# Other halves for the first exponentials, another order for the first loads, norms and masks, and turns of the identity at the start

## The chip, the cores and the metric

The kernel runs on one core of a Trainium2 chip. The metric is the time of one launch on the device in microseconds; times of single instructions come from one profiled execution of the same kernel.

## What is computed

Eight batches of x (256 channels by 512 positions) get a masked cross-attention with 16 heads of 16 channels against a context, and then a feed-forward part with a shared and eight routed experts. The reference, cut to what matters here (x and the context are indexed channel by position):

```python
q = einsum('oc,bct->bot', Wq, layernorm(x)) + bq      # k, v: the same with Wk, Wv on the context
dot = einsum('bhdt,bhds->bhts', q, k) / 4
mask = m[:, :, :, None] * m[:, :, None, :]
dot = mask * dot - (1 - mask) * 1e6
amap = softmax(dot, -1) * mask
x = x + einsum('bhts,bhds->bhdt', amap, v)
n = layernorm(x)
x = x + n + shared_expert(n) + routed_experts(n)      # two of eight experts a row
```

## The kernel before

The order of all work is written out by hand: each engine carries out its instructions in the order in which the code issues them, and waits where an operand or a buffer is not ready. Heads are taken in groups of four, four groups G to a batch, so G runs from 0 to 31. The products are in fp32.

**Setup (lines 115 to 194 and 1002 to 1026).** SyncE's queue (SP) issues the loads of x of batch 0 in two halves, then four small loads of the biases into bnat, then the context ctx. ScalarE's queue (ACT) issues Wq, the mask mb spread over all partitions, Wk and Wv. GpSimd (POOL) makes the identity ident and then a row of constants, the last of them nm, which takes the row maxima. `square` (line 1005) turns a weight matrix on TensorE, four turns of 128x128 into PSUM, and ACT copies it out. VectorE makes the layer norm of x in xm (`norm_stats` at 328, POOL raises the variance to -1/2 in rs, `start_norm` at 350 subtracts, scales and masks) and masks the context (`mask_context`, 341). `row_terms` (214) turns the biases and makes alpha and beta, with which `extra_rows` (385) gives each q and k its rows for bias and mask. `project_qk` (398) multiplies by the turned weights (psq, psk), and VectorE writes the two tiles of a pair of groups, one for each a in 0 and 1 (`rows`, line 409).

**Row maxima of group 0 (1034 to 1050).** `row_max` (421) makes the scores of 128 queries for half a group, that is for two heads, each on 32 rows of TensorE (L427), into PSUM tile s1 or s2, and VectorE takes the maximum (L429). Between the eight of them stand the turn of the mask (L1046), the router's weights (`load_router`, 253, L258) and seven tiles of shared weights (`weight_thunks`, 261, L272 and L284), each copied out by ACT. These and psq, psk take their PSUM from a pool with two buffers, tag mm; tags long, s1, s2 and av have one each. Then `take_max` (434) turns the maxima (psn, L438) and VectorE subtracts them from q (L439).

**Steps (1071 to 1146).** Each group has eight steps h. A step issues a `row_max` of the next group (L427 and L429, always into s1), `exp_scores` of this one (443: scores the other way round on two heads' rows, L450, into s2, and ACT's exponential, L452), at even h `attend` (457, av), and pieces of other work: `project_v` (360, psv, L372), `project_qk` of group pairs to come, loads, and later the feed-forward part. From step 6 of group 0 on, the maxima run LEAD = 2 steps ahead and the two matmul calls of a step are on different halves, that is on different rows of TensorE; in steps 1 to 5 of group 0 they run one ahead, and both calls are on the same half. In step 5 two maxima are issued to catch up.

## Time and profile before

| | us |
|---|---|
| median of 3 runs (911.38 to 923.37) | 920.09 |
| profiled execution | 898.62 |
| its span, first to last instruction | 896.8 |
| first k tile of group 0 ready (end of L411's third) | 14.5 |
| first row maximum's matmuls begin (L427) | 14.6 |
| q of group 0 less its maxima ready (L439) | 29.7 |
| matmuls of step 7 of group 0 end | 62.5 |

The three runs lie up to 1.3% apart. In the profile PE is TensorE's matmuls and PEld its weight loads, DVE is VectorE; L427 is line 427 of the kernel. "128x1024" is partitions by elements. The granted clock (PEclk) is TensorE's, as a share of full speed. A name left of "<-" is written, one right of it read; in a row of waits it is what ended the wait. Some rows from the beginning that the text uses:

| line, engine, operation | mean ns |
|---|---|
| L429 DVE maximum of 128x1024 | 1224 |
| L452 ACT exponential of 128x1024 | 1023 |
| L411 DVE q or k tile, 128x512 | 746 |
| L439 DVE subtraction from q, 128x512 | 688 |
| L393 ACT extra row, 128x512 | 810 |
| L344 POOL ctx times mask, 128x512 (later batches) | 1273 |
| L873 POOL issue of a load (later) | 609 |

### The profile page before, as it was taken

The page shows a single profiled execution, that of the slowest core. Times are in us where ns is not written, and L with a number is a line of the kernel's source. Part 1 is how long each engine was busy: PE and PEld are TensorE (multiplying, and loading weights), DVE is VectorE, ACT ScalarE, POOL GpSimd, SP SyncE. Part 2 cuts the span into 40 slices and gives each one's busy share as a digit, 9 for nine tenths or more (in the row PEclk, how much of TensorE's full clock was granted, in tenths as well). Part 3 has the DMA queues.
Part 4 walks back from the last instruction along what each step waited for, and adds up shares of the span by engine and source line. Part 5 has one row for each costly group of instructions (what it writes and reads, how often), then busy time and mean ns, then how long its engine had stood idle before and what let it go on. Part 6 is the DMA issues. An engine that isn't in the chain of part 4 may idle for free.

```text
span 896.8 us, 13356 instructions
## 1 busy us (share of the span) xinstructions
PE 844.5 (94%) x4947; PEld 340.3 (38%) x4947; DVE 580.9 (65%) x1083; ACT 364.3 (41%) x474; POOL 317.9 (35%) x393
## 2 busy tenths in 40 slices
PE   6998989999999999999999999999999998999996
PEld 3332323333333333333333333333333333555553
DVE  6556767776777677767776778577867753432356
ACT  3224444443444344434443444344434441455540
POOL 2105303552355235523552344234421121344431
PEclk9799999999999999999999999999999998999998
DMA  6119903212671255125512510020000001455455
GB/s 178 36 39 362 343 20 86 33 35 50 130 90 35 50 137 83 35 51 136 83 35 50 125 30 19 19 71 1 19 19 12 7 18 41 108 136 141 118 182 194
DMA packets 93004, 75.31 MB, mean 84 GB/s; under 512 B 60328, under 2 KB 81347, under 8 KB 92556
## 3 DMA queue, kind: packets, MB, share of 16 engines
q1 hardware_dynamic: 84956, 50.04, 21.3%
q0 software_dynamic: 7024, 23.37, 11.4%
q10 hardware_dynamic: 960, 1.05, 0.4%
q8 instruction: 40, 0.66, 0.3%
q14 instruction: 24, 0.20, 0.1%
HBM read 38.10 MB, written 40.79 MB: 88 GB/s over the span
## 4 chain that ended last, share of the span: by engine, by line
PE 72%; DVE 16%; issue 5%; POOL 3%; DMA 2%; SPq 1%; ACT 0%; DVEq 0%; ACTq 0%; POOLq 0%
PE s L427 23%; DVE nm L429 9%; PE av L465 9%; PE psy L956 4%; PE eu L793 4%; PE psq L404 4%; PE pu L905 3%; PE eg L793 3%; PE ey L823 3%; PE psk L404 3%; PE psv L372 3%; PE s L450 3%; PE pgu L905 3%; PE pg L905 2%; DVE q L411 2%
## 5 line engine op out<-in xcount | busy, mean ns | idle before, releaser
L452 ACT ACTIVATE e<-s 128x1024 f32<-128x1024 f32 x256 | 262.0, 1024 | 407.5 <-PE s L450 407.3
L429 DVE TENSOR_REDUCE nm<-s 128x2 f32<-128x1024 f32 x256 | 313.3, 1224 | 144.8 <-PE s L450 129.7
L427 PE MATMUL s<-k,q 32*128 32x512 f32 x1024 | 290.9, 644 | 24.3 <-DVE nm L429 21.3
L450 PE MATMUL s<-q,k 32*128 32x512 f32 x1024 | 289.9, 642 | 1.5 <-DVE q L439 0.8
L465 PE MATMUL av<-e,V 128*32 128x512 f32 x1024 | 137.5, 605 | 0.2 <-ACT e L452 0.2
L427 PEld LDWEIGHTS s<-k,q 32*128 32x128 f32 x1024 | 77.0, 184 | 131.7 <-DVE nm L429 110.4
L395 POOL TENSOR_SCALAR extra<-mb,alpha,beta 128x512 f32<-128x512 f32 x60 | 45.5, 763 | 175.9 <-DVE q L411 175.6
L337 POOL TENSOR_TENSOR rs<-ve,mhalf 128x1 f32<-128x1 f32 x32 | 18.2, 569 | 209.0 <-DVE ve L335 209.0
L450 PEld LDWEIGHTS s<-q,k 32*128 32x128 f32 x1024 | 77.3, 184 | 7.8 <-issue 5.6
L799 DVE SCALAR_TENSOR_TENSOR hz<-eth,eu 128x352 bf16<-128x352 f32 x45 | 23.4, 521 | 56.7 <-PE eu L793 49.3
L465 PEld LDWEIGHTS av<-e,V 128*32 128x32 f32 x1024 | 20.4, 108 | 98.1 <-issue 94.7
L956 PE MATMUL psy<-sdT,h 128*128 128x512 f32 (+1 forms) x96 | 52.3, 665 | 2.3 <-DVE h L917 2.3
L206 POOL DMA_INDIRECT xs<-xnb,at x30 | 29.9, 997 | 50.0 <-DVE at L654 27.2
L905 PE MATMUL pu<-xT,sguT 128*128 128x256 f32 x128 | 36.7, 403 | 0.0
L372 PE MATMUL psv<-WvT,ctx 128*128 128x256 f32 x128 | 36.7, 411 | 0.0
L793 PEld LDWEIGHTS <-late_ctx 128*128 128x128 bf16 x296 | 27.6, 97 | 23.4 <-issue 5.3
L905 PE MATMUL pg<-xT,sguT 128*128 128x256 f32 x128 | 35.3, 401 | 0.0
L793 PE MATMUL eu<-guT,late_ctx 128*128 x148 | 34.1, 310 | 0.9 <-ACT eth L798 0.8
L404 PE MATMUL psq<-xm,WqT 128*128 128x512 f32 x64 | 34.2, 660 | 0.0
L905 PE MATMUL pgu<-xT,sguT 128*96 128x256 f32 (+1 forms) x128 | 34.1, 393 | 0.0
L411 DVE SCALAR_TENSOR_TENSOR q<-psq,mine,extra 128x512 f32<-128x512 f32 x32 | 22.6, 746 | 15.6 <-PE psq L404 15.6
L206 POOL DMA_INDIRECT whose<-who,at x30 | 28.8, 961 | 9.1 <-issue 8.8
(200 smaller groups left out, 973.9 us busy)
## 6 DMA issues: line engine op xcount, KB each, us to landing
xs<-blank SPq DMA_DIRECT2D x7, 1920.0 KB, 13.2
ctx<-in_ctx_dram SPq DMA_DIRECT2D x8, 512.0 KB, 5.4
z<-zs SPq DMA_DIRECT2D x15, 256.0 KB, 4.5
x<-in_x_dram SPq DMA_DIRECT2D x7, 512.0 KB, 3.7
accd<-acc SPq DMA_DIRECT2D x12, 256.0 KB, 2.2
again<-accd POOLq DMA_DIRECT2D x12, 256.0 KB, 3.6
out_dram<-again POOLq DMA_DIRECT2D x12, 256.0 KB, 4.2
gu<-in_L_ffn_w_gate_dram POOLq DMA_DIRECT2D x8, 352.0 KB, 4.4
```

The source lines that it names most:

```text
L206: i = nc.gpsimd.indirect_dma_start(to[:, :], bass.IndirectOffsetOnAxis(ap=rows, axis=0), what, None, **bounds).ins
L372: nc.tensor.matmul(ps, ct[:, kc, sc * P : (sc + 1) * P], WvT[:, kc, :], start=(kc == 0), stop=(kc == 1))
L395: engine.tensor_scalar(t, S[b]["mb"], at, be, ALU.mult, ALU.add)
L404: nc.tensor.matmul(ps, W[:, kc, g // 2].rearrange("p j a d -> p (j a d)"), rhs[:, kc, :], start=(kc == 0), stop=(kc == 1),)
L427: nc.tensor.matmul(ps[:, jj, :], q[r, tci * P : (tci + 1) * P], k[r, :], start=True, stop=True)
L429: best = lambda: nc.vector.reduce_max(NM[G % 2][:, tci, c0 : c0 + 33 : 32], ps, axis=AX.X)
L450: nc.tensor.matmul(ps[:, jj, :], k[r, sc * P : (sc + 1) * P], q[r, :], start=True, stop=True)
L452: nc.scalar.activation(e, ps, AF.Exp)
L465: nc.tensor.matmul(AVT[G][32 * j : 32 * j + 32, :], V[:, sc, 2 * g + j // 2, j % 2 : j % 2 + 2, :].rearrange("p o d -> p (o d)"), et[j // ...
L793: nc.tensor.matmul(ps, xT[:, kc, :], weights_of(t, guT, m, kc, slice(None)), start=(kc == 0), stop=(kc == NKC - 1),)
L905: lambda kc=kc: nc.tensor.matmul(ps, sguT[:, m, kc, i0 : i0 + n + more], s["xT"][:, kc, :], start=(kc == 0), stop=(kc == NKC - 1))
L956: nc.tensor.matmul(t["y"], t["h"][:n, ic, tt * P : (tt + 1) * P], sdT[:n, ic, :], start=(ic == 0), stop=(ic == 2))
```

## The change

Five things, all at the beginning:

- The loads: ACT issues mb first, then Wk, Wq, Wv; SP issues x in halves and then ctx; the four loads of the biases go to POOL, after the identity. POOL's constants and nm are made after its part of the setup.
- Norms and masks: xm is made in one VectorE operation a half (subtract the mean, times mask), and ACT multiplies by rs. POOL masks one half of ctx, VectorE the other. `row_terms` is split: what does not need the biases is made in terms first, and `bias_terms` adds the biases.
- TensorE turns the identity into a PSUM tile that nobody reads (`busy`), 15 times at the start, and 2, 3 and 6 times between the first products.
- q's product for group pair 0 is issued in two parts with other work between. Of q and k the tiles for a = 0 are made first; q's for a = 1 comes after the first row maximum, k's after the second. The turned mask takes tag long. `project_v(0, 0)` is issued before the first exponentials; the others at steps 0, 5 and 7.
- Steps 1 to 5 of group 0: the exponentials take the other half than before (`half` for `1 - half`, steps 0 to 5), and the second maximum of step 5 comes at the end of that step.

```diff
+    nc.scalar.dma_start(out=S[0]["mb"], in_=mask[0, 0].partition_broadcast(P))
     for i in range(2):
         nc.sync.dma_start(out=S[0]["x"][:, i, :], in_=x[0, i * P : (i + 1) * P, :])
-    wq_nat = load_square(Wq)
-    nc.scalar.dma_start(out=S[0]["mb"], in_=mask[0, 0].partition_broadcast(P))
+    wk_nat, wq_nat = load_square(Wk), load_square(Wq)
+    nc.sync.dma_start(out=S[0]["ctx"], in_=src[0].rearrange("(h p) t -> p h t", p=P))
+    wv_nat = load_square(Wv)
...
-            nc.sync.dma_start(out=bnat[row : row + 2, :, a, :], in_=by_group[a])
-    nc.sync.dma_start(out=S[0]["ctx"], in_=src[0].rearrange("(h p) t -> p h t", p=P))
-    wk_nat, wv_nat = load_square(Wk), load_square(Wv)
+            nc.gpsimd.dma_start(out=bnat[row : row + 2, :, a, :], in_=by_group[a])
...
+    def busy(n):
+        for _ in range(n):
+            nc.tensor.transpose(idle, ident, ident)
+
+    idle = ps_av.tile([P, P], F32, tag="av", name="idle")
...
-    square(wq_nat, WqT, 0.25, ps_m, "mm")
-    start_norm(0, nc.vector)
+    def normed(i):
+        start_stats(0, i)
+        mv, rs = s0["stats", i]
+        xm = s0["xm"][:, i, :]
+        nc.vector.scalar_tensor_tensor(xm, s0["x"][:, i, :], mv[:, 0:1], s0["mb"], ALU.subtract, ALU.mult)
+        return lambda: nc.scalar.mul(xm, xm, rs)
+
+    row_terms()
+    busy(15)
     square(wk_nat, WkT, 1.0, ps_s, "s1")
-    row_terms()
-    mask_context(0, nc.vector)
-    wv = turn_square(wv_nat, ps_s, "s2")
-    extra_rows(0, 0, nc.scalar)
+    square(wq_nat, WqT, 0.25, ps_s, "s2")
+    busy(2)
+    scaled = normed(0)
+    scaled()
+    q_part, q_rows = project_qk(0, 0, True)
+    k_part, k_rows = project_qk(0, 1, True)
+    q_part(0)
+    scaled = normed(1)
+    bias_terms()
+    nc.gpsimd.tensor_mul(s0["ctx"][:, 0, :], s0["ctx"][:, 0, :], s0["mb"])
+    nc.vector.tensor_mul(s0["ctx"][:, 1, :], s0["ctx"][:, 1, :], s0["mb"])
+    scaled()
+    wv = turn_square(wv_nat, ps_s, "s1")
+    extra_rows(0, 0, nc.scalar, (0,))
+    extra_rows(0, 1, nc.scalar, (0,))
+    busy(3)
+    q_part(1)
+    q_rows(0)
+    for kc in range(2):
+        k_part(kc)
+    k_rows(0)
+    busy(6)
+    extra_rows(0, 0, nc.scalar, (1,))
     nc.scalar.copy(WvT, wv)
-    extra_rows(0, 1, nc.scalar)
-    project_qk(0, 0)
-    k_rows = project_qk(0, 1, True)
+    extra_rows(0, 1, nc.scalar, (1,))
...
             best = row_max(1, 0, 0, "s1", True)
             take_max(0)
+            best()
+            project_v(0, 0)
+            continue
         best()
         if r == 0:
-            k_rows(1)
-            pt = ps_m.tile([P, B * 4], F32, tag="mm", name="pt")
+            q_rows(1)
+            pt = ps_m.tile([P, B * 4], F32, tag="long", name="pt", bufs=1)
...
+        elif r == 1:
+            k_rows(1)
             load_router()
-        elif r != 7:
+        if r not in (0, 7):
             weights.pop(0)[1]()
...
-                lead = LEAD if G or h > 5 else LEAD - 1
-                for R in range(8 * (G + 1) + h + lead, 8 * (G + 1) + h + lead + (2 if G == 0 and h == 5 else 1)):
-                    if (G or h) and R // 8 < last:
-                        row_max(R // 8, (R % 8) // 2, R % 2)
-                exp_scores(G, st, 1 - half, "s2" if R // 8 < last else ("s1", "s2")[h % 2])
+                short = G == 0 and h < 6
+                R = 8 * (G + 1) + h + LEAD - short
+                if (G or h) and R // 8 < last:
+                    row_max(R // 8, (R % 8) // 2, R % 2)
+                exp_scores(G, st, half if short else 1 - half, "s2" if R // 8 < last else ("s1", "s2")[h % 2])
...
-                if b == 0 and g == 0 and h in (0, 2, 5, 7):
-                    project_v(0, (0, 2, 5, 7).index(h))
+                if b == 0 and g == 0 and h in (0, 5, 7):
+                    project_v(0, (0, 5, 7).index(h) + 1)
...
+                if G == 0 and h == 5:
+                    row_max(1, 3, 1)
```

More of the change, by code (lines that the diff above doesn't have):

```diff
@@ L125, in xattn_ffn_kernel @@
     }
+    nc.scalar.dma_start(out=S[0]["mb"], in_=mask[0, 0].partition_broadcast(P))
     for i in range(2):
         nc.sync.dma_start(out=S[0]["x"][:, i, :], in_=x[0, i * P : (i + 1) * P, :])
-    wq_nat = load_square(Wq)
-    nc.scalar.dma_start(out=S[0]["mb"], in_=mask[0, 0].partition_broadcast(P))
+    wk_nat, wq_nat = load_square(Wk), load_square(Wq)
+    nc.sync.dma_start(out=S[0]["ctx"], in_=src[0].rearrange("(h p) t -> p h t", p=P))
+    wv_nat = load_square(Wv)
     bnat = five.tile([2 * NG, 4, 2, HD], F32, tag="acc", name="bnat")
     nc.vector.memset(bnat, 0.0)
+    ident = const.tile([P, P], F32, name="ident")
+    make_identity(nc, ident)
     for side, bias in enumerate((bq, bk)):
@@ L135, in xattn_ffn_kernel @@
             row = NG * side + 2 * a
-            nc.sync.dma_start(out=bnat[row : row + 2, :, a, :], in_=by_group[a])
-    nc.sync.dma_start(out=S[0]["ctx"], in_=src[0].rearrange("(h p) t -> p h t", p=P))
-    wk_nat, wv_nat = load_square(Wk), load_square(Wv)
-    ident = const.tile([P, P], F32, name="ident")
-    make_identity(nc, ident)
+            nc.gpsimd.dma_start(out=bnat[row : row + 2, :, a, :], in_=by_group[a])
     rowis = const.tile([P, 32], F32, name="rowis")
@@ L158, in xattn_ffn_kernel @@
     rank = const.tile([P, E], F32, name="rank")
-    for e in range(E):
-        nc.gpsimd.memset(rank[:, e : e + 1], float(E - e))
     identb = const.tile([P, P], BF16, name="identb")
-    nc.gpsimd.tensor_copy(identb, ident)
     before = const.tile([P, P], BF16, name="before")
-    make_upper_triangular(nc, before, 1.0, diag=False)
     onesb = const.tile([P, P], BF16, name="onesb")
-    nc.gpsimd.memset(onesb, 1.0)
     base0 = const.tile([P, E], F32, name="base0")
     upto = const.tile([P, E, E], F32, name="upto")
-    nc.gpsimd.memset(upto, 0.0)
-    for e in range(E):
-        nc.gpsimd.memset(base0[:, e : e + 1], float(ROWS * e))
-        nc.gpsimd.memset(upto[:, e, : e + 1], 1.0)
     eights = const.tile([P, 8], F32, name="eights")
-    for i in range(8):
-        nc.gpsimd.memset(eights[:, i : i + 1], float(8**i))
     thirds = const.tile([P, 3], F32, name="thirds")
-    for i in range(3):
-        nc.gpsimd.memset(thirds[:, i : i + 1], float(P ** (i - 1)))
     ncol = const.tile([P, 1], F32, name="ncol")
-    nc.gpsimd.iota(ncol, [[0, 1]], channel_multiplier=P, allow_small_or_imprecise_dtypes=True)
     tv = const.tile([P, NT], F32, name="tv")
-    nc.gpsimd.iota(tv, [[1, NT]], channel_multiplier=0, allow_small_or_imprecise_dtypes=True)
     place0 = const.tile([P, 2, 2], F32, name="place0")
-    nc.gpsimd.iota(place0, [[ROWS, 2], [P, 2]], channel_multiplier=1, allow_small_or_imprecise_dtypes=True)
     HZ = []
@@ L192, in xattn_ffn_kernel @@
         nm = const.tile([P, NSTEP, P], F32, name=f"nm{i}")
-        nc.gpsimd.memset(nm, 0.0)
         NM.append(nm)
@@ L212, in scatter @@
         before.append(i)
+    terms = const.tile([P, 2, 2, NG // 2], F32, name="terms")
     def row_terms():
-        pt = ps_m.tile([P, 2, 2, NG // 2], F32, tag="mm", name="pt")
-        nc.tensor.transpose(
-            pt.rearrange("p s a c -> p (s a c)"), bnat.rearrange("r j a d -> r (j a d)"), ident[: 2 * NG, : 2 * NG]
-        )
-        nc.vector.tensor_scalar(alpha[:, 0], pt[:, 0], 0.25, None, ALU.mult)
-        nc.vector.tensor_copy(alpha[:, 1], pt[:, 1])
+        nc.vector.memset(terms, 0.0)
         for a in range(2):
@@ L228, in row_terms, with bias_terms @@
                 nc.vector.scalar_tensor_tensor(
-                    alpha[:, 0, a], R.to_broadcast([P, 2]), big, alpha[:, 0, a], ALU.mult, ALU.add
+                    terms[:, 0, a], R.to_broadcast([P, 2]), big, terms[:, 0, a], ALU.mult, ALU.add
                 )
-            nc.vector.tensor_sub(alpha[:, 1, a], alpha[:, 1, a], R1.to_broadcast([P, 2]))
+            nc.vector.tensor_sub(terms[:, 1, a], terms[:, 1, a], R1.to_broadcast([P, 2]))
             nc.vector.tensor_add(beta[:, 1, a : a + 1], beta[:, 1, a : a + 1], R2)
+    def bias_terms():
+        pt = ps_m.tile([P, 2, 2, NG // 2], F32, tag="long", name="pt", bufs=1)
+        nc.tensor.transpose(
+            pt.rearrange("p s a c -> p (s a c)"), bnat.rearrange("r j a d -> r (j a d)"), ident[: 2 * NG, : 2 * NG]
+        )
+        nc.vector.scalar_tensor_tensor(alpha[:, 0], pt[:, 0], 0.25, terms[:, 0], ALU.mult, ALU.add)
+        nc.vector.tensor_add(alpha[:, 1], pt[:, 1], terms[:, 1])
     WqT = wts.tile([P, 2, 2, 4, 2, HD], F32, name="WqT")
@@ L383, in xattn_ffn_kernel, with extra_rows @@
     EXTRA = {}
-    def extra_rows(G, side, engine):
+    def extra_rows(G, side, engine, which=(0, 1)):
         b, g = divmod(G, NG)
         if True:
-            for a in range(2):
+            for a in which:
                 t = three.tile([P, T], F32, tag="extra", name=f"extra{side}_{G + a}")
@@ L396, in extra_rows, with project_qk @@
                 EXTRA[G + a, side] = t
-    def project_qk(G, side, one_now=False):
+    def project_qk(G, side, by_parts=False):
         b, g = divmod(G, NG)
@@ L402, in project_qk, with product @@
         ps = ps_m.tile([P, T], F32, tag="mm", name="psk" if side else "psq")
-        for kc in range(2):
+        def product(kc):
             nc.tensor.matmul(
@@ L414, in rows @@
             QK.setdefault(G + a, []).append(t)
-        rows(0)
-        if one_now:
-            return rows
-        rows(1)
+        if by_parts:
+            return product, rows
+        for i in range(2):
+            product(i)
+        for a in range(2):
+            rows(a)
     def row_max(G, tci, half, tag="s1", later=False):
@@ L999, in spread @@
         assert not items
-    for i in range(2):
-        start_stats(0, i)
+    def busy(n):
+        for _ in range(n):
+            nc.tensor.transpose(idle, ident, ident)
+    idle = ps_av.tile([P, P], F32, tag="av", name="idle")
     def square(nat, dst, scale, *where):
@@ L1014, in square @@
                     nc.scalar.mul(at, by_row, scale)
-    square(wq_nat, WqT, 0.25, ps_m, "mm")
-    start_norm(0, nc.vector)
-    square(wk_nat, WkT, 1.0, ps_s, "s1")
-    row_terms()
-    mask_context(0, nc.vector)
-    wv = turn_square(wv_nat, ps_s, "s2")
-    extra_rows(0, 0, nc.scalar)
-    nc.scalar.copy(WvT, wv)
-    extra_rows(0, 1, nc.scalar)
-    project_qk(0, 0)
-    k_rows = project_qk(0, 1, True)
+    s0 = S[0]
+    s0["xm"] = one.tile([P, 2, T], F32, tag="xm", name="xm0")
+    def normed(i):
[4 more added lines that the diff above has]
+        return lambda: nc.scalar.mul(xm, xm, rs)
@@ new lines, in xattn_ffn_kernel @@
+    extra_rows(0, 0, nc.scalar, (0,))
[8 more added lines that the diff above has]
+    extra_rows(0, 0, nc.scalar, (1,))
+    nc.scalar.copy(WvT, wv)
+    extra_rows(0, 1, nc.scalar, (1,))
+    for nm in NM:
+        nc.gpsimd.memset(nm, 0.0)
+    for e in range(E):
+        nc.gpsimd.memset(rank[:, e : e + 1], float(E - e))
+    nc.gpsimd.tensor_copy(identb, ident)
+    make_upper_triangular(nc, before, 1.0, diag=False)
@@ new lines, in xattn_ffn_kernel @@
+    nc.gpsimd.memset(onesb, 1.0)
+    nc.gpsimd.memset(upto, 0.0)
+    for e in range(E):
+        nc.gpsimd.memset(base0[:, e : e + 1], float(ROWS * e))
+        nc.gpsimd.memset(upto[:, e, : e + 1], 1.0)
+    for i in range(8):
+        nc.gpsimd.memset(eights[:, i : i + 1], float(8**i))
+    for i in range(3):
+        nc.gpsimd.memset(thirds[:, i : i + 1], float(P ** (i - 1)))
+    nc.gpsimd.iota(ncol, [[0, 1]], channel_multiplier=P, allow_small_or_imprecise_dtypes=True)
+    nc.gpsimd.iota(tv, [[1, NT]], channel_multiplier=0, allow_small_or_imprecise_dtypes=True)
@@ L1029, in xattn_ffn_kernel @@
+    nc.gpsimd.iota(place0, [[ROWS, 2], [P, 2]], channel_multiplier=1, allow_small_or_imprecise_dtypes=True)
     mnat = five.tile([B * 4, P], F32, tag="acc", name="mnat")
```

## The prediction

> **What bounds the kernel now.** I read the page first: TensorE is busy for 94% of the span and carries the chain.

> ```profile
> span 896.8 us, 13356 instructions
> PE 844.5 (94%) x4947; PEld 340.3 (38%) x4947; DVE 580.9 (65%) x1083; ACT 364.3 (41%) x474; POOL 317.9 (35%) x393
> PEclk9799999999999999999999999999999998999998
> ```

> The second digit of PEclk, 7, is the one low slice near what the change touches. The order of instructions before and after agrees from step 7 of group 0 on, so later work only shifts, and what the change gives or costs is decided before 62.5 us, where that step's matmuls end. The chain of waits for that stretch:

> ```profile
> 1.74 5.25 DMA wnat<-in_L_xattn_Wk_dram
> ...
> 9.38 2.55 PE psq L404 x4
> 11.93 1.73 PE psk L404 x4
> ...
> 17.15 0.59 PE pt L272 x4
> 17.74 1.06 PE s L427 x4
> ...
> 38.31 3.59 PE psq L404 x4
> ```

> psk at 11.93 takes 1.73 us, the same shape at 38.31 takes 3.59: TensorE's clock is halved there. The busy time by stretches, cut at the clock's own changes:

> ```profile
> 7.51:10.93 3.42, 3.42 (x11) 2.03 (x11) 3.35 (x20) 1.85 (x6) 0.22 (x1) 1.00 0.79 225
> 14.34:17.75 3.41, 2.89 (x19) 1.26 (x19) 2.18 (x4) 0.37 (x2) 0.00 (x0) 1.00 0.24 74
> 27.99:31.41 3.42, 2.54 (x12) 1.04 (x12) 1.91 (x3) 0.53 (x1) 0.00 (x0) 1.00 0.00 0
> 31.41:34.82 3.41, 3.41 (x10) 1.47 (x8) 1.36 (x2) 0.49 (x1) 0.00 (x0) 0.50 0.02 5
> 34.82:38.23 3.41, 3.41 (x8) 0.88 (x6) 1.70 (x3) 0.00 (x0) 0.00 (x0) 0.50 0.00 0
> 38.23:41.65 3.42, 3.42 (x6) 1.18 (x4) 0.00 (x0) 1.02 (x1) 0.00 (x0) 0.50 0.00 0
> 51.89:55.30 3.41, 2.08 (x16) 0.60 (x12) 1.69 (x2) 0.85 (x1) 0.00 (x0) 1.00 0.00 0
> 55.30:58.71 3.41, 3.41 (x12) 1.18 (x6) 1.23 (x1) 1.02 (x1) 0.00 (x0) 0.50 0.00 0
> ```

> (After the stretch: PE, PEld, DVE, ACT, POOL busy, clock, DMA.) The clock is 0.50 for 10.24 + 3.41 us. It shows 1.00 before 10.93 too, but psq's first half ran at half speed (2.55 against 1.73). In 34.82:38.23 PE is 100% busy and the clock stays low, so busy time does not raise it. I therefore weigh each matmul's streaming time (0.43 us for a 512-column pass, psk's 1.73 / 4) by the share of the 128 rows it uses; a call of L427 or L450 streams 0.85 us on half the rows, a square of four turns 0.43 on all, psv or av 0.85, psq or psk 1.71. The eight stretches then have 0.89, 0.39, 0.34, 0.67, 0.46, 0.95, 0.36, 0.79. The clock rose after 0.89, 0.95 and 0.79, not after 0.67; it fell after 0.34 and 0.36, not after 0.39. My reading, an inference from this trace: under about 0.37 in one such window halves the clock, over about 0.73 restores it.

> [...] all changes lie multiples of 3.41 us apart. [...] 7.51:10.93 is more than half turns and was followed by a rise, so here I count them. [...]

> **First loads, norms, masks.** Removed from the path: four bias loads ahead of ctx on SP (ctx issued at 6.21, now about 1.6), a VectorE operation per half of x (xm in one of about 0.70, ACT does the scaling, instead of 0.63 + 0.68), half of the ctx mask. The biases go to POOL, four issues at about 0.6 (row L873: 609 ns), 1.3 to 3.7 us, hidden by the wait for x0 (3.92), before rs needs POOL at 5.1. POOL's constants move behind its ctx half (1.27 us, row L344); nm is then set by about 11 us, before its first use near 16: nothing. If ctx were late, that cover would go and cost up to 1 us. Added: Wq is now third on ACT's queue. Loads landed 5.0 to 5.4 us after issue; with 0.5 MB more in the same time I put Wq at 7.0, Wv and ctx at 8.4. Then turns 0.6, ACT's four copies 0.78, the scaling of xm half 0 (0.8, behind those copies on ACT): first product at 9.3. TensorE's queue from there: 0.86 + bias turn 0.13 + Wv 0.6 + three turns 0.4 + 3 x 0.86 = 4.6, then k's row operation 0.75: k0 ready at T = 14.7, against 14.5 before. Where the clock is still low, 17. I take +0.7; bounds -1.0 (loads 1 us earlier) and +2.5. Three things wait beside this path: alpha (VectorE) for the bias turn, now behind the first product, 10.4; the extra rows on ACT for alpha, 3 x 0.8 to 13; and WvT's copy (0.56) behind them, which frees s1 for the first row maximum, 13.6. That is 1.1 us before T; were alpha later by more, WvT would end last.

> **Fifteen turns at the start.** Cold, 0.21 each (1.11 for four, less the last one's tail): 1.33 to 4.6, waiting on the identity only. They fill idle time and end before Wk: cost nothing, 0 to 0.3. They can raise the clock by 4 to 6.4 us on about three quarters of grids (2.5 us of activity within a window).

> **q's second row behind the first maximum.** This is the step I weigh most. Before, both q rows preceded k0, and after it VectorE ran maximum 1.24, k row 0.75, maximum. Now it is maximum, q row, maximum, k row. The router's turn waits for that q row (it takes psq's buffer, since mask columns moved to "long"), weight turn 1 waits for ACT's copy of the router, and row maximum 2 is queued behind both on TensorE. So: r0 T to T+1.1, r1 to T+2.2, q row done T+3.15, router to T+3.5, weight turn T+3.75 to 4.35, r2 T+4.4 (before T+3.2): +1.25 us, bounds 0.9 and 1.5. In those 3.4 us TensorE has 0.43 + 0.43 = 0.86 weighted: 0.25. Every window that begins between T-0.4 and T+3.2 lies below 0.37; that is 3.6 us against a grid of 3.41, so nearly every grid has one. **The clock should halve at T+3 to T+6.4**, where before it fell here only on grids whose window began between 12.7 and 14.1.

> At half rate the row maxima stay at about 0.57 (0.43 + 0.43 weighted, doubled, in 2.9 us): it cannot rise. Each step grows from 1.65 to 2.93: r2 to r7, 6 x 1.28 = 7.7; weight turn 7, the first maximum of group 1 and psn, 0.32 + 0.85 + 0.43 = 1.6; psv0, now here, 0.85. Sum 10.2.

> **Project_v(0, 0) moved ahead of the first exponentials.** psv 1.06 hides under the subtraction from q (0.70): +0.35, and 1.06 less later.

> **Halves exchanged.** For h = 1 to 4 L427 and L450 now use different rows. Before: 1.06 + 0.86; together as at 62 us: 1.12; 4 x 0.8 = 3.2. With psv0 gone and VectorE (1.24 behind each pair, one s1 buffer) in the way of some, I walk the queue from q's end to step 7: 26.8 before at full clock (32.8 measured; the halved clock took 6.0), 23.9 after. Gain 2.9, bounds 1.5 and 3.5. psv1, the first pair and psq follow each other at over 0.85, so here the clock rises again, after one or two windows: 1.7 to 3.4 lost, 2.5 taken.

> **The sum.** q ready: 29.66 + 0.7 + 1.25 + 0.35 + 10.2 = 42.2; step 7 at 42.2 + 23.9 + 2.5 = 68.6, against 62.5: +6.1 us. On the profiled execution 898.6 becomes 904.7. The median of the runs is 920.1, 21.5 above the profile. Their spread of 12 us is about what an early fall costs before (10.2, less the 2 us or so of the later one): if the median run had the profile's grid, after is 926.2; if it had the early fall (8.3 more), 917.9. I take the middle, 922.

> **Rivals.** B, the clock holds: router and turn start sooner than I think, or activity is counted otherwise. For it: 14.34:17.75 held at 0.39, near the mark. Then step 7 ends at 14.7 + 1.25 + 15.1 + 0.35 + 23.9 = 55.3: -7.2, or -15.5 from a run with the early fall: 904.6 to 912.9. C, slower: the clock is never raised before step 8. A's 12.7 us lost in some 27 cold ones are 0.47 each; without the cold the change gives 6.0 + 0.6 here, so 2% slower needs (18.4 + 6.6) / 0.47 = 53 cold us, from 17 to 70. Pairs and psq at over 0.85 speak against, the low clock from the start on a quarter of grids for it. With half of it, 932 to 940. D, the exchange and the earlier loads do little because VectorE ends last, and the clock falls alike in both: 912 to 919.

> **Numbers.** A 0.60 (own range 912 to 932), B 0.22, C 0.08, D 0.10. The measurement tells about 2% from no change. Under 901.7 goes half of B and a fifth of D: 0.13; over 938.5 half of C and a little of A: 0.06; within 2%: 0.81. 907 leaves out half of B, 934 most of C.

> **What shows it.** Clock 0.50 beginning 17.5 to 21 us; r2's matmuls 4.4 us after k0; 2.9 us per row maximum; L427 and L450 overlapping from step 1; q ready near 42; step 7 at 66 to 71. Wrong if the clock reads 1.00 through the row maxima, if Wq lands before 6 us, or if the runs' scatter hides a cause outside the first 63 us.

## The result

The changed kernel takes 926.36 us (median of 20 runs, 924.03 to 934.18); the kernel before, on the same chip, 920.92 us (20 runs, 911.38 to 935.6). The ratio is 1.0099, 95% interval 1.0078 to 1.012: no change by the measure of 2%, but the interval lies wholly above 1, so the change costs about 1%. A second comparison (below, `after_again`) gives 906.3 against 900.45 us, ratio 1.0082 (1.0065 to 1.0099). Both ratios leave out runs more than 1.5% above the fastest of their kernel, which in the second comparison drops the runs of the kernel before near 908 us.

The prediction was 922.0 us (907 to 934), within 2% the likeliest. Two numbers have to be kept apart from the start. The first 94 us cost 9.1 us more in the profiled execution after than in the one before, and that belongs to the change. Another 22 us or so of difference between these two profiles (928.4 against 896.8 us of span) lie between 200 and 760 us; the changed kernel run again shows that they do not belong to it.

### The profile page after: what moved, and what is told of

Same layout as the page of the kernel before. It is cut to its first block, busy times and chain, and to the rows that moved or that the text cites. A ratio compares the mean times of both kernels' runs of the same rounds, so it can differ in the third digit from the quotient of the medians.

```text
span 928.4 us, 13402 instructions
## 1 busy us (share of the span) xinstructions
PE 863.5 (93%) x4961; PEld 350.1 (38%) x4973; DVE 579.5 (62%) x1081; ACT 365.7 (39%) x476; POOL 322.8 (35%) x398
## 4 chain that ended last, share of the span: by engine, by line
PE 68%; DVE 17%; issue 6%; POOL 3%; DMA 2%; another core or an unknown queue 2%; ACT 2%; SPq 0%; DVEq 0%; ACTq 0%; POOLq 0%
PE s L418 22%; DVE nm L420 10%; PE av L456 8%; PE psy L947 4%; PE eu L784 4%; PE psq L393 4%; PE s L441 3%; PE eg L784 3%; PE pu L896 3%; PE ey L814 3%; PE psk L393 3%; PE pgu L896 2%; PE pg L896 2%; DVE q L400 2%; PE psv L360 2%
## 5 line engine op out<-in xcount | busy, mean ns | idle before, releaser
L418 PE MATMUL s<-k,q 32*128 32x512 f32 x1024 | 295.8, 657 | 28.9 <-DVE nm L420 26.1
L441 PE MATMUL s<-q,k 32*128 32x512 f32 x1024 | 291.5, 646 | 6.1 <-DVE nm L420 2.7
L418 PEld LDWEIGHTS s<-k,q 32*128 32x128 f32 x1024 | 78.4, 187 | 136.8 <-DVE nm L420 113.8
L441 PEld LDWEIGHTS s<-q,k 32*128 32x128 f32 x1024 | 77.3, 184 | 15.5 <-issue 6.5
L947 PE MATMUL psy<-sdT,h 128*128 128x512 f32 (+1 forms) x96 | 51.3, 654 | 2.0 <-DVE h L908 2.0
L784 PEld LDWEIGHTS <-late_ctx 128*128 128x128 bf16 x296 | 27.5, 97 | 23.1 <-issue 5.2
L784 PE MATMUL eu<-guT,late_ctx 128*128 x148 | 34.1, 310 | 1.0 <-ACT eth L789 0.8
L393 PE MATMUL psq<-xm,WqT 128*128 128x512 f32 x64 | 33.7, 648 | 1.1 <-ACT xm L1020 1.1
L896 PE MATMUL pgu<-xT,sguT 128*96 128x256 f32 (+1 forms) x128 | 34.1, 392 | 0.0
L896 PEld LDWEIGHTS pu<-xT,sguT 128*128 128x128 f32 x128 | 22.7, 196 | 25.8 <-issue 22.9
L393 PE MATMUL psk<-ctx,WkT 128*128 128x512 f32 x64 | 32.1, 625 | 0.0
```

What stands on the lines that cost most here:

```text
L393: nc.tensor.matmul(ps, W[:, kc, g // 2].rearrange("p j a d -> p (j a d)"), rhs[:, kc, :], start=(kc == 0), stop=(kc == 1),)
L418: nc.tensor.matmul(ps[:, jj, :], q[r, tci * P : (tci + 1) * P], k[r, :], start=True, stop=True)
L441: nc.tensor.matmul(ps[:, jj, :], k[r, sc * P : (sc + 1) * P], q[r, :], start=True, stop=True)
L784: nc.tensor.matmul(ps, xT[:, kc, :], weights_of(t, guT, m, kc, slice(None)), start=(kc == 0), stop=(kc == NKC - 1),)
L896: lambda kc=kc: nc.tensor.matmul(ps, sguT[:, m, kc, i0 : i0 + n + more], s["xT"][:, kc, :], start=(kc == 0), stop=(kc == NKC - 1))
L947: nc.tensor.matmul(t["y"], t["h"][:n, ic, tt * P : (tt + 1) * P], sdT[:n, ic, :], start=(ic == 0), stop=(ic == 2))
```

## The profile after

Span, TensorE and its granted clock, from the page of the changed kernel:

```profile
span 928.4 us, 13402 instructions
PE 863.5 (93%) x4961; PEld 350.1 (38%) x4973; DVE 579.5 (62%) x1081; ACT 365.7 (39%) x476; POOL 322.8 (35%) x398
PEclk7599999999999999999998999999999999999998
```

TensorE still bounds the kernel: busy for 93% of the span, 68% of the chain that ended last. PEclk has 7 and 5 in its first two slices where the kernel before had 9 and 7, and no other digit below 8. The other engines' shares moved by 3 points at most, so the place to look at is the start. The chain of waits there (start, length, what):

```profile
1.65 8.15 DMA wnat<-in_L_xattn_Wq_dram
...
12.44 2.07 PE psq L393 x2
...
18.11 2.18 PE psk L393 x4
...
25.14 0.66 PE pt L260 x4
25.79 2.01 PE s L418 x4
...
52.63 1.93 PE psq L393 x4
```

(L393, L400, L418, L441, L246, L260 are the former L404, L411, L427, L450, L258, L272.) The chain begins with Wq, 8.15 us on its way, where before it began with Wk at 5.25. One half of psq takes 2.07 us and one row maximum (L418) 2.01, where two of psk's four passes took 0.87 in the kernel before (half of 1.73) and a row maximum 1.06: about half speed, at a granted clock of 0.50. At 52.63 the full product takes 1.93, where the same product took 3.59 before: the clock is back ahead of it now, and was still halved at it then. The busy time by stretches, cut at this run's own clock changes (columns as in the prediction, the last two the DMA engines' share and GB/s):

```profile
12.06:15.48 3.42, 3.04 (x7) 1.51 (x8) 0.73 (x3) 1.47 (x3) 3.32 (x44) 0.50 0.24 74
15.48:18.89 3.41, 3.41 (x9) 1.86 (x8) 0.77 (x2) 2.16 (x4) 0.04 (x1) 0.50 0.43 135
18.89:22.31 3.42, 3.07 (x19) 1.52 (x17) 0.83 (x2) 0.81 (x1) 0.00 (x0) 1.00 0.00 0
22.31:25.72 3.41, 1.11 (x13) 0.74 (x8) 3.21 (x4) 0.37 (x2) 0.00 (x0) 1.00 0.25 77
25.72:29.13 3.41, 3.41 (x11) 1.57 (x12) 1.69 (x2) 0.83 (x2) 0.00 (x0) 0.50 0.50 135
46.20:49.61 3.41, 3.41 (x14) 2.00 (x12) 2.37 (x4) 0.00 (x0) 0.00 (x0) 0.50 0.00 0
49.61:53.02 3.41, 3.15 (x19) 1.29 (x14) 2.09 (x4) 1.32 (x2) 0.00 (x0) 1.00 0.00 0
```

In 22.31:25.72 VectorE is busy for 3.21 us and TensorE for 1.11, and the next stretch has a clock of 0.50. Weighted by rows as in the prediction, these stretches have 0.73, 1.0, 0.90, 0.125, 0.55, 0.86 and 0.80: a rise after 1.0 and 0.86, none after 0.73, the fall after 0.125. TensorE's timeline shows what it waited for (the bracket: idle before, and releaser):

```profile
21.28 1.14 PE L418 MATMUL s<-k,q 32*128 32x512 f32 x8 [0.35 <-DVE k L400]
22.21 0.19 PE L1090 MATMUL pt<-ident,mnat 32*128 32x32 f32 x1
24.45 0.41 PE L246 MATMUL pt<-ident,wnat 8*128 8x8 f32 x4 [2.03 <-DVE q L400]
25.14 0.66 PE L260 MATMUL pt<-ident,wnat 128*128 128x128 f32 x4 [0.28 <-ACT sguT L247]
25.72 2.08 PE L418 MATMUL s<-k,q 32*128 32x512 f32 x4
```

The first line holds the matmuls of the first two row maxima (x8): they use different halves of the rows and take 1.14 us together. Then the router's turn (L246) stands for 2.03 us on q's second row (L400), which is behind the first maximum on VectorE. The clock falls at 25.72, and the third maximum starts in that moment. In the kernel before, the router's turn waited 0.30 us, and the third maximum came 3.1 us behind the start of the first (14.56):

```profile
16.01 0.22 PE L258 MATMUL pt<-ident,wnat 8*128 8x8 f32 x1 [0.30 <-ACT mcol L1047]
...
17.67 1.13 PE L427 MATMUL s<-k,q 32*128 32x512 f32 x4
```

The milestones that I use below are the first exponential and the exponential of step 8 (the ninth, first of group 1). Before: 30.9 and 65.2 us; after: 50.0 and 74.3. The 9.1 us stay the same to the forty-ninth exponential (171.2 and 180.3).

## The experiments

Twelve runs in four comparisons, each on a chip of its own and with runs of the kernel before on the same chip. The chips differ: the kernel before has 899.64, 900.45, 919.4 and 923.68 us on them. So times are compared within a comparison, and milestones of the first 94 us across all. Medians are of 20 or more runs, but of 8 in `e4_halves_only`, 4 in `e6_start_before`, 5 in `e7_loads_undone` and 6 in `e8_more_turns`. One program profiled twice differs too: the changed kernel's milestones lie at 50.0 and 74.3 in its first profile, at 49.3 and 73.5 in `after_again`.

| run | us, median | before, same chip | ratio (95%) | first exponential | exponential of step 8 |
|---|---|---|---|---|---|
| e1_turns_gap | 897.47 | 899.64 | 0.998 (0.9964 to 0.9995) | 38.3 | 63.5 |
| e2_qrow_first | 905.39 | 899.64 | 1.0052 (1.003 to 1.0073) | 48.9 | 73.2 |
| e3_ctx_later | 904.79 | 899.64 | 1.0059 (1.0042 to 1.0076) | 47.2 | 71.5 |
| before_again | 900.09 | 899.64 | 1.0027 (1.0001 to 1.0053) | 41.4 | 73.8 |
| after_again | 906.3 | 900.45 | 1.0082 (1.0065 to 1.0099) | 49.3 | 73.5 |
| e4_halves_only | 893.24 | 900.45 | 0.9921 (0.988 to 0.9962) | 31.2 | 59.6 |
| e5_no_turns | 906.07 | 900.45 | 1.0076 (1.0059 to 1.0094) | 48.1 | 74.3 |
| e6_start_before | 890.39 | 900.45 | 0.988 (0.9821 to 0.9939) | 31.4 | 58.2 |
| e7_loads_undone | 934.37 | 919.4 | 1.0177 (1.0105 to 1.0248) | 46.7 | 71.1 |
| e8_more_turns | 907.15 | 919.4 | 0.9891 (0.9826 to 0.9957) | 31.4 | 56.6 |
| e10_before_turns | 919.94 | 919.4 | 1.0009 (0.9983 to 1.0036) | 31.5 | 64.5 |
| e11_mended | 914.74 | 923.68 | 0.994 (0.9911 to 0.997) | 35.8 | 61.1 |

The row `before_again` is the kernel before set against itself, and its interval lies just above 1. So a ratio of 0.998, as that of `e1_turns_gap`, is no gain over the kernel before.

**Does the halved clock come from the idle window?** Theory: the clock follows the share of activity in a window. Rival: the maxima are slow because of the waits themselves, or the clock falls for another cause.

```
         elif r == 1:
             k_rows(1)
+            busy(12)
             load_router()
+            busy(4)
```

> The changed kernel with 12 turns of the identity put on TensorE between the second row maximum and the router's turn, and 4 between the router's turn and the first weight turn, where TensorE waited in the changed kernel (22.5 to 24.45 and 24.6 to 25.14 us). Theory (the clock follows the share of row-weighted activity in a 3.41 us window): the window that had 0.125 and was followed by the halved clock gets about 1.3 us more activity, a share of about 0.5, so the clock holds, a row maximum step takes 1.65 us and not 2.9, the first exponential comes near 39 us (50.0 in the changed kernel), the step-8 exponential near 62 to 64 (74.3), and the time falls by 9 to 12 us against the changed kernel. Rival (the row maxima are slow because of the waits for VectorE, or the clock falls for another cause than idleness): the first exponential stays at 49 to 51 us and the time at about 926.

Measured: first exponential 38.3, step 8 at 63.5, 897.47 us, 8.8 under `after_again` (on another chip; the kernel before differs by 0.8 between the two). Its TensorE timeline at the same place:

```profile
21.60 1.53 PE L996 MATMUL idle<-ident 128*128 128x128 f32 x12
23.70 0.41 PE L246 MATMUL pt<-ident,wnat 8*128 8x8 f32 x4 [0.57 <-DVE q L400]
24.04 0.66 PE L996 MATMUL idle<-ident 128*128 128x128 f32 x4
24.53 0.60 PE L260 MATMUL pt<-ident,wnat 128*128 128x128 f32 x4
25.06 1.13 PE L418 MATMUL s<-k,q 32*128 32x512 f32 x4
```

The router's turn still waits for q's row, and the third maximum still starts 4.5 us behind the start of the first, as in the changed kernel (4.4). Only the standing still is gone: the window has 0.60 in place of 0.125, the maxima take 1.13 us and not 2.08, a step 1.6 and not 3.0, and nothing falls from 17.3 us to 754. The rival fell.

**Is it the place of q's row?** The rows of q and k are put back as before:

```
+    extra_rows(0, 0, nc.scalar, (1,))
+    q_rows(1)
     k_rows(0)
     busy(6)
-    extra_rows(0, 0, nc.scalar, (1,))
...
         if r == 0:
-            q_rows(1)
+            k_rows(1)
...
         elif r == 1:
-            k_rows(1)
             load_router()
```

> The changed kernel with q's second row and k's second row back where they were before: q's second row ahead of k's first, k's second behind the first maximum, so that the router's turn does not wait behind a maximum. Theory: k0 is ready about 0.75 us later, but the third row maximum comes 3.2 us after it and not 4.6, the window behind it holds about 0.4 to 0.65 of activity, and the clock holds on most grids: first exponential near 40 us. If the grid lies badly and the clock falls, near 51. Rival (the place of q's row does not matter): the clock falls as in the changed kernel, first exponential at 50 to 51 us, time about 927.

Measured: the clock falls (25.06), first exponential 48.9. The expectation missed, and the timeline says why:

```profile
20.91 1.14 PE L418 MATMUL s<-k,q 32*128 32x512 f32 x8 [0.28 <-DVE k L400]
21.88 0.39 PE L246 MATMUL pt<-ident,wnat 8*128 8x8 f32 x4
24.09 0.66 PE L260 MATMUL pt<-ident,wnat 128*128 128x128 f32 x4 [1.82 <-DVE k L400]
```

The router's turn no longer waits, but the first weight turn now waits for k's second row, which holds psk's buffer: the mask columns' turn was on the other tag, so the buffers went round otherwise than before. The wait of 2.03 us became one of 1.82 a place further. Moving one row was not enough here; giving TensorE something to do was (16 turns in `e1_turns_gap`, share 0.60).

**Why does it start late?** In `e3_ctx_later` the biases are back on SP's queue ahead of ctx; in `e7_loads_undone` all first loads stand in the order of before (Wq, mb, Wk, Wv on ACT; x, biases, ctx on SP), with the computing as changed.

> The changed kernel with the four bias loads back on SP's queue ahead of ctx, so that ctx is issued at about 6 us and not at 1.6. Theory (x0 and Wq came late, 6.0 and 9.85 us, because ctx's 512 KB share the DMA engines with them): x0's statistics begin near 4 us, Wq's turns at 7 to 8, the first row maximum at 16 to 18 us and not 21.3, the clock still falls behind the second maximum, and the first exponential comes 3 to 5 us sooner. Rival (Wq is late because it is third on its own queue, whatever ctx does): Wq's turns stay at 9.5 to 10 us and the first row maximum at 20.5 to 22.

> The changed kernel with the order of its first loads as before: Wq, mb, Wk, Wv on ACT's queue, x, the four biases and ctx on SP's, none on POOL's; the order of the computing stays the changed one. Theory (x0 and Wq came late because mb, Wk and ctx share the DMA engines with them): x0's statistics begin near 4 us and not at 6.0, Wq's turns follow Wk's at about 8, the first product at about 10, the first row maximum's matmuls at 18 to 19 (21.3 in the changed kernel, 14.5 before), and the clock falls behind the second maximum all the same; 902 to 904 us. What stays of the lateness, some 4 us, is then the order of the computing (first product at the low clock, Wv's turns and idle turns ahead of its second half). Rival (the loads' order is no part of it): first row maximum at 20.5 or later.

Measured for the first: x0's statistics at 5.65 (not near 4, as expected), Wq's turns at 8.20 (9.82 in `after_again`), k's first row at 17.7 (19.7), first exponential at 47.2, that is 2.0 sooner and not 3 to 5. For the second: statistics at 3.76, k's first row at 17.3. From TensorE's timeline of the second (its lines are numbered one lower than the changed kernel's):

```profile
7.34 1.31 PE L231 MATMUL pt<-ident,wnat 128*128 128x128 f32 x8 [2.53 <-DMA wnat<-in_L_xattn_Wk_dram]
10.15 2.07 PE L392 MATMUL psq<-xm,WqT 128*128 128x512 f32 x2 [1.08 <-ACT xm L1019]
18.16 1.14 PE L417 MATMUL s<-k,q 32*128 32x512 f32 x8 [0.35 <-DVE k L399]
```

Wk's and Wq's turns now run in one group of eight at 7.34, and the first maximum starts at 18.2 and not 21.3. So the loads make 3.1 of the 6.7 us by which the start is late against the kernel before (14.56); against `after_again`, where the first maximum starts at 20.61, they make 2.4. Most of that is there in `e3_ctx_later` already, where ctx and the biases alone are moved (first maximum at 18.6). There Wq comes sooner, but x0 comes at its old time only when mb and Wk stand as before, too (5.65 in e3, 3.76 in e7). What stays, 3.6 us, goes with the rest of the change and was not taken apart further than by the turns below. The timeline shows half of psq at the low clock (2.07), then Wv's turns and three idle ones (12.36 to 13.9) ahead of the second half. The time of `e7_loads_undone` does not follow: 934.37 us, five runs from 927 to 938 (whether that is 2% slower than the kernel before stays unclear), though its first 94 us are 3.2 us shorter than the changed kernel's. Its profiled execution is the shortest of the five (927.16), and there the stretch from the 17th to the last exponential, 683.9 us, is no longer than in `e10_before_turns` on the same chip (686.9). What makes the other four longer is open.

**What are the 26 turns worth?** `busy` issues nothing:

> The changed kernel without any of its 26 turns of the identity (15, 2, 3 and 6). Theory: the first fifteen raise the clock at 5.2 us for one window in which TensorE waits for Wk and Wq, and it falls again at 8.7, so they give nothing; the later ones bring the rise that came at 18.9, at most one window sooner, 1 to 2 us at the first row maximum. First row maximum at 21 to 24 us, the clock still halved through the row maxima, time within 2 us of the changed kernel's on this chip. Rival (the turns are what keeps the start from being slower): 4 us or more on top.

Measured: 906.07 against 906.3 us, first maximum 1.0 us sooner (VectorE's reduction at 20.81, not 21.84), and one more fall at 67.1 us. Where the change put them, the turns are worth nothing in time. In the first profile after, the fifteen at the start did raise the clock (5.24, after a window of 0.82 that held nothing but turns), and it fell again at 8.65, after 0.125, while TensorE waited for Wk. In `after_again` they lay across two windows (0.73 and 0.21) and raised nothing; without turns the first rise comes at 15.93.

**What is the exchange of halves worth alone?**

```
-                lead = LEAD if G or h > 5 else LEAD - 1
-                for R in range(8 * (G + 1) + h + lead, 8 * (G + 1) + h + lead + (2 if G == 0 and h == 5 else 1)):
...
+                short = G == 0 and h < 6
+                R = 8 * (G + 1) + h + LEAD - short
...
+                exp_scores(G, st, half if short else 1 - half, "s2" if R // 8 < last else ("s1", "s2")[h % 2])
...
+                if G == 0 and h == 5:
+                    row_max(1, 3, 1)
```

> The kernel before with only the exchange of halves in the first six steps (and the last row maximum of group 1 at the end of step 5). The prediction's step: from the subtraction of the row maxima to the exponential of step 8, 36.2 us in the kernel before with 10 us of it at the low clock, the exchange takes 2.9 us off at full clock, and the window with 0.34 of activity at 52 to 55 us may be gone, another 2: time 894 to 897 us where the kernel before has 899.6. Rival (VectorE's row maxima through one buffer set the pace, 2.45 to 2.9 us a step as in the run with turns in the gap, so overlapping the matmuls of a step gives little): 898 to 900.

Measured: 893.24 us, ratio 0.9921; step 8 at 59.6 and not 65.2. The two matmul groups of a step now run on each other, seen in TensorE's timeline:

```profile
37.90 0.70 PE L427 MATMUL s<-k,q 32*128 32x512 f32 x2
37.91 0.70 PE L450 MATMUL s<-q,k 32*128 32x512 f32 x2
38.43 0.59 PE L427 MATMUL s<-k,q 32*128 32x512 f32 x2
38.44 0.59 PE L450 MATMUL s<-q,k 32*128 32x512 f32 x2
```

That is 1.12 us for both (37.90 to 39.02). From the subtraction's end to step 7 it takes 27.1 us in place of 32.9. If the overlap gives the 2.9 that were predicted, the other 2.9 are the first fall of the clock, which lasts one window (32.0 to 35.4) and not three: that window has a share of 0.77, where the kernel before had 0.67 in its own. This split is worked out and not measured. The second fall, which might have gone, stayed (52.5). The rival fell.

**Whose are the 22 us after 200 us?** The two kernels once more, unchanged:

> The kernel before, unchanged, for a second profiled execution: its first was 898.6 us where its runs have a median near 921. If the spread comes from the grid of the clock in the first 63 us (as the prediction supposed), the first 63 us take 5 to 10 us longer here and the rest the same 834 us. If it comes from later waits, as the six exponentials that wait 3.6 us for TensorE in the changed kernel between 200 and 760 us suggest, the stretch from the 17th to the last exponential takes 670 to 685 us here and not 660.8.

> The changed kernel, unchanged, beside runs of the kernel before on the chip that gave 899.6 us for it. Theory (the six later waits of 3.6 us and the level of 921 to 926 us belong to where the program ran; the change itself costs what the first 94 us show, 9.1 us against the kernel before on its commonest grid): 904 to 909 us, the stretch from the 17th to the last exponential 659 to 664 us as in the kernel before, no exponential waiting 3.6 us. Rival (the later waits come with the changed program): 920 us or more, that stretch near 685 us.

Measured: `before_again` was profiled at 908.56 us; its clock fell at 16.99 for 34.1 us, and the 17th exponential came 8.6 us later than in the first profile, while the stretch from the 17th to the last took 663.1 us (660.8). `after_again`: 906.3 us, that stretch 661.8, where the first profile after had 685.2, and no exponential waits. In the first profile after, the chain showed this about once in a batch, here in the second:

```profile
206.54 1.02 ACT e L443
207.56 3.62 another core or an unknown queue
...
211.26 1.03 ACT e L443
```

Two exponentials stand 4.7 us apart that are 2.7 apart elsewhere. The eight exponentials of this profile that come over 4.2 us behind the one before them make some 16 of the 24 us by which the stretch is longer. The kernel before with only twelve turns near its first maxima shows the same on the chip where the kernel before takes 919.4:

> The kernel before with nothing changed but 12 turns of the identity near the first maxima (6 ahead of the first, 3 ahead of the router's turn, 3 behind the second). Theory (its runs at 904 and 908 us are those whose clock falls between the first two maxima and the second step): those runs are gone, all lie at 893 to 900 us; the fall at 28 to 31 us (share 0.36, behind the last row maxima) can still come. Rival (the 908 us runs have another cause): they stay, about one run in four.

Measured: 919.94 us, the same as the kernel before there (911.7 to 931.9, so the missing of early falls could not be seen in the times: inconclusive). Its profile has no fall between the first maxima and one at 31.7, as expected. And its chain at the same place of the program:

```profile
203.71 2.04 PE psv L372 x4
205.75 0.02 issue
205.77 1.24 DVE nm L429
```

psv takes 0.87 us at 198.75, and VectorE's maximum and the exponential (205.89) both wait there. Nine exponentials of this run come over 4.2 us behind the one before them, 6 to 8 in each of the four other profiles from comparisons at that level (the changed kernel's first among them), none in the eight profiles from the two chips at about 900, nor in the first of the kernel before. So these waits do not come with the change. They go with the chip, or with its state at that hour: each chip served in one comparison only, so the two can't be told apart. What delays TensorE by about 2 us there is open. POOL issues its row scatters at that time, but it does so in `after_again` too, where nothing waits; and the instruction queue's transfers do not coincide (in the first profile after, none between 379.5 and 402.5 us, where one of these waits begins at 392.4).

**Does it add up, and is there something better?** `e6_start_before` keeps the start of the kernel before, and takes the exchanged halves, V's early product and 12 turns:

```
+    busy(6)
...
             nc.scalar.copy(mcol, pt)
+            busy(3)
             load_router()
+        elif r == 1:
+            busy(3)
+            weights.pop(0)[1]()
```

> The kernel before with its own loads, norms and masks, and of the change only the exchanged halves and V's first product ahead of the first exponential, and with turns of the identity where TensorE waits near the first maxima: 6 ahead of the first, 3 ahead of the router's turn, 3 behind the second maximum. Theory: the first row maximum at 14.7 us, the clock holds on every grid, the first exponential near 31.5, the exponential of step 8 near 57 to 58 (65.2 in the kernel before, 63.5 with turns in the changed kernel): 889 to 892 us in nearly all runs, without the spread of 894 to 908 that the kernel before shows. Rival (the clock falls later all the same, or turns delay the maxima): 897 us or more.

Measured: 890.39 us (889.36 to 892.26), step 8 at 58.2, as expected but for one fall at 51.3 us. `e8_more_turns` adds 14 + 7 turns around Wq's and fills the gap at the end of step 5:

```
                 if G == 0 and h == 5:
                     row_max(1, 3, 1)
+                    fill = ps_m.tile([P, P], F32, tag="long", name="fill", bufs=1)
+                    for _ in range(8):
+                        nc.tensor.transpose(fill, ident, ident)
```

> The run that kept the kernel before's start and took the exchanged halves (890.4 us) with more turns: 14 ahead of Wq's turns and 7 behind them, so that the clock rises one window sooner (6.9 and not 10.3 us), and 8 at the end of step 5, where the window with 0.37 of activity was followed by a fall at 51.3. Theory: first product 0.6 us shorter, no low clock between 10 and 740 us, the exponential of step 8 at 55.5 to 56.5 (58.2): 887 to 889 us. Rival (turns ahead of Wk and in step 5 push the real work back by as much): 890 to 892.

Measured: step 8 at 56.6 (expected 55.5 to 56.5), 1.5 sooner than in `e6_start_before`, all from step 5; the early turns raise the clock at 6.04 but k's first row comes at 13.81 as without them, since psq still waits for VectorE (1.09 us at 9.97). Its chip is the one of 919.4, so the time of 907.15 us can't be set against the 887 to 889 expected; the ratio 0.9891 is that of `e6_start_before` within the intervals. Both are about 1% under the kernel before, and so under the changed one, too.

The last run mends the changed kernel itself, in its loads and in the gap:

> The changed kernel with two mends together: the order of its first loads as before, and the 12 + 4 turns of the identity around the router's turn; the 2 and 3 idle turns ahead of q's two products are left out. Theory (the start and the fall of the clock are two separate costs that add up, and the exchange of halves is a separate gain): k's first row at 16.7 us (17.26 with the loads alone, 19.6 with the turns alone), no fall of the clock behind the second maximum, the first exponential at 35 to 36 us and that of step 8 at 60 to 61 (63.5 with the turns alone, 71.1 with the loads alone, 58.2 with the start of the kernel before). Time 893 to 896 us where the kernel before has 900, some 6 us under it where later waits make it 919. Rival (the two interact: an earlier start moves the grid so that another window falls): the exponential of step 8 at 63 us or later.

Measured: first exponential 35.8 and step 8 at 61.05, 12.5 us sooner than in `after_again`. The turns alone gave 10.0 (73.5 to 63.5) and the loads alone 2.4 (to 71.1): they add up. k's first row came at 17.1, not 16.7: dropping the idle turns gave nothing on top. The ratio of 0.994 is 5 to 6 us under the kernel before, as expected; the medians of all runs lie 8.9 apart.

## Why the prediction was right

It was right in its verdict and in its mechanism. Its number lies near the measured one with the help of luck: the median was to move by 1.9 us and moved by 5.4, and the first steps were to cost 6.1 us and cost 9.1.

1. **Clock behind the second maximum: right.** Predicted to halve at T+3 to T+6.4 for nearly every grid (T is the moment at which k's first row is ready); it fell at T+4.6 (T = 21.14), and in the profiles of `after_again`, e2, e3, e5 and e7 as well. The share was lower than thought, 0.125 and not 0.25, because the first two maxima run at once (1.14 us for both); I had put them one behind the other. The maxima then took 2.85 to 3.05 us each (predicted 2.93). T to q ready took 26.1 us, predicted 27.5.
2. **Router behind q's row: right.** 2.03 us of waiting; the third maximum 4.6 us after T, predicted 4.4.
3. **Halves exchanged: right to a tenth at full clock.** q ready to step 7 takes 23.94 us in e1, predicted 23.9. The 26.8 us that it was set against were run by no kernel at full clock, so the gain of 2.9 itself is not measured. In the first profile after, with the clock back from 49.6, it took 24.5, so the return of the clock cost 0.5 and not 2.5: the window 46.20:49.61 already held the end of psn, psv and the first pair, a share of 0.86, and the clock rose behind it.
4. **First loads: the term that was mis-sized.** The prediction took +0.7 with bounds of -1.0 and +2.5, and T = 14.7, at most 17. T was 21.14. Wq was put at 7.0 and its turns began at 9.85; x0, taken as unchanged at 3.92, came at 6.00. The lines of the kernel before, then those after:

```profile
3.92 0.69 DVE L332 BATCH_NORM_STATS2 st<-x 128x6 f32<-128x512 f32 x1 [2.23 <-DMA x<-in_x_dram]
4.70 1.09 PE L244 MATMUL pt<-ident,wnat 128*128 128x128 f32 x4 [4.70 <-DMA wnat<-in_L_xattn_Wq_dram]
...
6.00 0.69 DVE L320 BATCH_NORM_STATS2 st<-x 128x6 f32<-128x512 f32 x1 [2.94 <-DMA x<-in_x_dram]
9.85 1.11 PE L232 MATMUL pt<-ident,wnat 128*128 128x128 f32 x4 [1.71 <-DMA wnat<-in_L_xattn_Wq_dram]
```

Loads were added up by bytes, as if the ones issued first kept their time. In the first profile after, the busy share of the 16 DMA engines is 0.99 to 1.09 in each microsecond from 5 to 9 us, at 350 to 398 GB/s. In e3 and e7 x0 and Wq, which stand first on the path, come sooner when ctx, mb and Wk are issued as before (x0 at 5.65 and 3.76, Wq at 8.20 and in the group of eight from 7.34); so it was these that held them up. e7 gives 3.1 us to the loads. The other 3.6 come with the order of computing at the low clock; the prediction had 17 for a low clock, 2.3 more than for a raised one, but took +0.7.

5. **Fifteen turns: cost right, worth wrong.** They end at 4.81, ahead of Wk (7.47), and so hold nothing up, and they raised the clock within the first 5.4 us in five of the seven profiles that have them (not in `after_again` and e1), about as often as predicted; but it fell again one window later each time, so in the first profile after the first half of q's product took 2.07 us, at a clock of 0.50.
6. **The sum.** Step 7 ends at 71.7 where 68.6 was predicted: +6.4 from T, -1.4 from the maxima, -1.9 from the clock's return. Together +3.1: so some +9.1 and not +6.1 on the profile's scale.
7. **From the profile to the runs: right number, wrong reason.** The 21.5 us between the profiled execution of the kernel before and its median were put down to the grid. The grid does spread the kernel before (nearly all runs within 894 to 909 us on one chip, `before_again` 8.6 us later at the 17th exponential after an early fall, 8.3 had been worked out), but that is too little for 21.5. The later waits would account for them: the first profile (898.62 us, no such wait) lies under all 20 runs of its kernel in the first comparison (911.38 at least) and at the level of the chips with 900. On which chip it was taken is not on record. That one of the two figures averaged for the forecast, 926.2, met the measured 926.36 is luck: 6.1 us stood in it for 9.1. The prediction named this as what would make it wrong ("if the runs' scatter hides a cause outside the first 63 us"), and it did hide one. What lies outside the span explains nothing of the 21.5 us: nearly every run's time is its span plus some 1.8 us, that of the profile too (898.62 and 896.8). That the median differs by 5.4 us and not 9.1 is explained in part: some runs of the kernel before have the early fall as well, while all 20 of the changed kernel lie within 904.9 to 909.1 in `after_again`.

Rival B (the clock holds) is what e1 shows once the gap is filled; C did not come, since the clock rose at 49.61, right behind the window with psv and the first pair (0.86); D was wrong on the exchange, which alone gave 0.8% (e4).

## What to carry to other kernels

Before moving an operation off TensorE's path, ask what TensorE does in that moment: here a place with a wait of 2 us cost 10, because a window with almost no work (share 0.125) was followed by seven at a clock of 0.50 (23.9 us), and sixteen idle turns around that place bought them back, while the 26 turns of the change, fifteen of them ahead of another wait, bought nothing (906.3 us with them, 906.07 without). Load first what the path needs first, and hold back large transfers that nobody waits for yet: here the order of the loads made 2.4 to 3.1 us. Split a change into its parts when its total is near nothing: here the exchange of halves alone gives 0.8% and the new start takes more than that away.

## What the runs showed of the hardware

The changes of the granted clock, between 1.00 and 0.50, lie whole multiples of 3.41 us apart up to 740 us: 20.48, 10.24, 13.65 and 3.41 us for the first ones of the first profile before, 3.41, 10.24, 6.83 and 23.89 for those of the first after. Where these windows lie differs between executions, which the prediction's "nearly every grid" took for granted: less multiples of a sixth of 20.48 us, the changes at 31.41 (before), 16.99 (`before_again`), 25.72 (after) and 25.06 (`e2_qrow_first`) leave 0.69, 3.34, 1.83 and 1.17 us.

The two row maxima of different halves take 1.14 us together where one takes 1.13. And one and the same program, the kernel before, takes 900 us on two chips and 919 and 924 on two others. In the profiles from the latter, exponentials come about 2 us late behind TensorE, about once a batch.
